# Copies of the transposed k, in a linear-attention and mixture-of-experts kernel: from VectorE to ScalarE

## The chip, the cores and the metric

The kernel runs on one core of one Trainium2 chip. The metric is the time of one execution on the device, in microseconds (us). The engines are named as the profile names them: PE (TensorE, the matmuls), PEld (its weight loads), DVE (VectorE), ACT (ScalarE), POOL (GpSimd) and SP (SyncE, which here only issues transfers). Each engine carries out its own instructions in the order in which they stand in its program, and waits on semaphores for what other engines have to deliver. PSUM is the memory into which PE writes, in eight banks; SBUF is the large on-chip memory.

## The reference

Four batches of 512 tokens with 256 channels pass through two blocks, all in float32, each with a residual and a layer norm in front.

```python
q = k = x @ Wqk + bqk                  # 16 heads of 16 channels
v, u  = silu(x @ Wv + bv), silu(x @ Wu + bu)
q, kh = elu(heads(q)), elu(heads(k))
kv    = einsum('bhnd,bhne->bhde', kh, vh)
out   = einsum('bhnd,bhde->bhne', q, kv)
x     = x + (u * layernorm(out)) @ Wo + bo
...
gate  = einsum('bsd,de->bse', layernorm(x), gate_kernel)   # 8 experts, the best 2 of them
inter = silu(h0) * h1                                      # hidden width 512
x     = x + einsum('bse,bsem,emd->bsd', combine, inter, wo_kernel)
```

The attention has no softmax over the tokens: each head's k and v are first multiplied over all 512 tokens of a batch into a 16 by 16 matrix kv, and q is then multiplied by it. q and k are the same numbers here.

## The kernel before, in words

**Attention.** `attention(b)` is a generator with twelve stages for one batch; the four batches start four stages apart and run interleaved, the later batch's stage first. The stages that the text speaks of, with their lines:

- The layer norm of x (`layernorm`, L247 to L286): statistics with L252 and L253, a chain of ten tiny DVE operations for the reciprocal root (L255 to L272, each waiting for the one before), then four normalizations, L284 on DVE for tokens of even blocks and L280 on ACT for odd ones. POOL then adds bo to x (L305).
- x is transposed on PE (L292) and copied by ACT (L297).
- k and q: PE multiplies (L317), ACT takes the exponential (L322), DVE makes elu of it (L323, L324). The result kT has channels on the partitions and tokens along the free dimension.
- v and the gate logits (L346, L351, L354, L358), and u (`project`, L334, L338).
- kn, k with tokens on the partitions: PE transposes kT (L391) into a PSUM bank, two blocks of 128 tokens at a time, and **L394 copies the bank to SBUF**. There are two such copies a batch, eight in all, each of 128 partitions by 512 floats. For batch 0 the gate's own small products stand in the same stage (L380 to L410).
- kv: PE multiplies kn and v (L421, with kn as weights), DVE masks it (L429).
- the attention output o: L442 on PE, L446 on ACT; its layer norm, with the same lines as the first; transposed (L292), scaled by ACT (L457) and multiplied by u on DVE (L461).
- the output projection L469 on PE, the residual L473 on DVE, and the result's transfer to the output, issued by ACT (L476).
- the routing: the two best experts (L498, L499, L502, L508), the third layer norm into hn, whose rows POOL doubles (L511), the exponential of the second weight (L516), then L518 to L520.
- the places: PE counts the tokens of each expert up to here (L524, L526), DVE makes row numbers (L530, L533) and counts (L535), and POOL scatters hn to the DRAM buffer xg with eight indirect transfers a batch (L539).

**Experts.** When two batches are routed, `plan` (L658) makes the list of the first blocks of 128 rows. For a block, SP fetches the rows from xg (L715), which has to wait until the scatters of the batches it depends on have landed; PE transposes them (L726), ACT copies (L729), expert weights at a place known only at run time are staged by ACT and DVE copies (L741), and PE multiplies (L759, then silu L843 and product L778, then L798). DVE weights the result (L809), and POOL adds it to the output with an indirect transfer (L819). The third expert matrix, w2, is loaded by SP (L174) into the arena slots that attention used, each load as soon as the slot's last reader is done.

**What sets the order.** The source's order is not the order on the engines: the tile framework schedules the instructions of each engine by its own estimate of their costs, and inserts the waits. So moving one operation to another engine can also reorder others. PSUM banks are handed out in turn by `bank`, and a bank's next writer waits for its last reader.

```python
for t0 in range(0, NT, 2):                              # L387
    ps = bank([P, 2, E], f"knp_{b}_{t0}")
    for t in range(t0, t0 + 2):
        for c in range(EC):
            nc.tensor.transpose(ps[:, t - t0, bass.ts(c, P)], kT[:, c, bass.ts(t, P)], ident)
    nc.vector.tensor_copy(kn[:, t0 : t0 + 2, :], ps)    # L394
```

Of the kernel before, what the change touches and what calls it, by code (L numbers as in the profile page):

```python
# [32 lines left out]
def kernel(  # L33
# [32 lines left out]
    nc = tc.nc  # L66
# [29 lines left out]
    def bank(shape, name, n=1):  # L96

        at = (used[0] + used[0] % n) % BANKS
        used[0] = (at + n) % BANKS
        if n == 2:  # L100
            return banks[:, at : at + 2, 0 : shape[2]]
        tile_ = banks[:, at, 0 : math.prod(shape[1:])]
        if len(shape) == 3:
            tile_ = tile_.rearrange("p (a b) -> p a b", a=shape[1])
        return tile_
# [9 lines left out]
    def att(tag):  # L115

        i = turns[tag] % COUNT[tag]
        turns[tag] += 1
        if tag == "kv":
            return arena[:, AT[tag], bass.ts(i, E)]  # L120
        return arena[:, AT[tag] + i, :]
# [177 lines left out]
    def attention(b):  # L299
# [14 lines left out]
        for c in range(EC):  # L314
            ps = bank([P, N], f"qp_{b}_{c}")
            for k in range(EC):
                nc.tensor.matmul(  # L317
                    ps, lhsT=wqk_sb[:, k, bass.ts(c, P)], rhs=xT[:, k, :],
# [23 lines left out]
        for t0 in range(0, NT, 2):  # L342
            ps = bank([P, 2, E + NE], f"vp_{b}_{t0}", 2)
# [18 lines left out]
        if b == 0:  # L362

            ps = bank([P, NE], "gate_sum")
            for k in range(EC):
                nc.tensor.matmul(
                    ps, lhsT=ones, rhs=wv_sb[:, k, E:], start=(k == 0), stop=(k == EC - 1)
# [9 lines left out]
            ps = bank([P, EC, E], "woTp")  # L377
# [8 lines left out]
        kn = att("tok").rearrange("p (t e) -> p t e", t=NT)  # L386
# [4 lines that stand above are left out]
                    nc.tensor.transpose(  # L391
                        ps[:, t - t0, bass.ts(c, P)], kT[:, c, bass.ts(t, P)], ident
                    )
            nc.vector.tensor_copy(kn[:, t0 : t0 + 2, :], ps)  # L394
        if b == 0:

            ps = bank([P, EC + 1, NE], "wog")
# [18 lines left out]
        ps = bank([P, EC, HALF], f"kvp_{b}")  # L416
# [21 lines left out]
        for t0 in range(0, NT, 2):  # L438
            ps = bank([P, 2, E], f"op_{b}_{t0}")
# [25 lines left out]
        for t0 in range(0, NT, 2):  # L465
            ps = bank([P, 2, E + NE], f"ap_{b}_{t0}", 2)
# [26 lines left out]
        ps = x1[:, :, E:]  # L493
# [364 lines left out]
    W2_AT = 9  # L858
    begin = [0, 4, 8, 12]
    running = [attention(b) for b in range(B)]  # L860
    ready = []
    for at in range(max(begin) + STAGES + 1):
# [37 lines left out]
    with tc.If(many > USUAL - EARLY):  # L900
# [7 lines left out]
        for name, some in (  # L908
# [8 lines left out]
            for b in range(B):  # L917
# [10 lines left out]
                for t in range(NT):  # L928
                    ps = bank([P, E], f"spread_{name}_{b}_{t}")
                    for k in range(NT):  # L930
                        nc.tensor.matmul(
                            ps, lhsT=at[k][:, bass.ts(t, P)], rhs=state["made"][:, k, :],
# [49 lines left out]
```

## Time and profile before

| What | Value |
|---|---|
| Median of 3 runs | 327.46 us (326.52 to 327.5) |
| The profiled execution | 326.6 us |
| its span, first to last instruction | 324.8 us |
| mean granted TensorE clock | 0.964 |
| PE busy | 293.6 us (90%) |
| DVE busy | 157.0 us (48%) |
| ACT busy | 127.1 us (39%) |
| POOL busy | 121.7 us (37%) |
| the chain that ended last | PE 73%, DVE 19%, ACT 3% |

The profile is of one execution, and all its times are us from the start of its span. A row of a group gives the source line, the engine, the operation, the tile written and the tiles read, and how often; then the durations. In an answer in order of time, the first column is the start and the second the duration, and a bracket tells how long the engine had stood and what it waited for. Two operations of one engine can overlap by their pipelines, so an operation's duration is a little more than the time for which it keeps its engine from the next. The chain of work that ended last is followed back from the last instruction: at each step to what released it, or to the instruction before it on its engine; its second column is the time that the step adds to the chain.

Attention fills the first 115 us or so, and the experts' matmuls the rest. The share of DVE and ACT over the whole span says little about attention, where DVE is the fullest engine for long stretches.

### The profile page before, as it was taken

To read this page: it belongs to the slowest core of one execution; us is meant where nothing else is said; L and a number is where in the kernel's file an instruction comes from. 1 tells how busy PE (TensorE), PEld (TensorE's weight loads), DVE (VectorE), ACT (ScalarE), POOL (GpSimd) and SP (SyncE) were. 2 spreads that over 40 slices of the span, in tenths; PEclk is the share of its full clock that TensorE was granted. 3 is DMA by queue.
4 is the path that set the end of the run, shared out by engine and by line. 5 is a ranking of instruction groups with operands and counts; after the bars stand their busy time and mean duration, and the time that the engine had idled before them with its cause. 6 is when DMAs were issued, how large, how long until landed. Compare 5 with 4: busy or idle time off the path is not lost.

```text
span 324.8 us, 5819 instructions
## 1 busy us (share of the span) xinstructions
PE 293.6 (90%) x1948; PEld 235.9 (73%) x1948; DVE 157.0 (48%) x567; ACT 127.1 (39%) x203; POOL 121.7 (37%) x161
## 2 busy tenths in 40 slices
PE   0999999899794599999999999999999999999970
PEld 0567677576663389899974456758999999999960
DVE  5653979979968466843221232332232323233320
ACT  2465566357341835524212144334242424343200
POOL 5340041176461553752331343323343224332321
PEclk9999999999996579999999999999999999999996
DMA  6999403054168450734433122232323433322121
GB/s 199 329 387 385 174 2 109 22 163 163 36 227 266 123 197 9 225 83 64 68 52 54 18 34 35 33 44 33 59 29 63 60 55 61 58 33 34 18 34 20
DMA packets 27731, 32.98 MB, mean 102 GB/s; under 512 B 3249, under 2 KB 22577, under 8 KB 27697
## 3 DMA queue, kind: packets, MB, share of 16 engines
q1 hardware_dynamic: 19056, 21.73, 21.4%
q0 software_dynamic: 6528, 8.72, 16.3%
q10 hardware_dynamic: 2112, 2.10, 1.9%
q8 instruction: 18, 0.29, 0.4%
q14 instruction: 17, 0.13, 0.1%
HBM read 20.53 MB, written 12.01 MB: 100 GB/s over the span
## 4 chain that ended last, share of the span: by engine, by line
PE 73%; DVE 19%; ACT 3%; issue 1%; DMA 1%; POOL 0%; POOLq 0%; DVEq 0%; ACTq 0%
PE banks L759 28%; PE banks L798 19%; PE banks L767 7%; PE banks L469 4%; DVE st L252 4%; PE banks L317 3%; PE banks L726 3%; PE banks L292 2%; PE banks L346 2%; DVE x L473 1%; PE banks L334 1%; PE banks L421 1%; PE banks L785 1%; DVE mv L253 1%; ACT arena L457 1%
## 5 line engine op out<-in xcount | busy, mean ns | idle before, releaser
L759 PE MATMUL banks<-arena 128*128 128x128 f32 x896 | 108.8, 275 | 0.1
L759 PEld LDWEIGHTS banks<-arena 128*128 128x128 f32 x896 | 106.2, 192 | 1.6 <-ACT arena L741 0.3
L729 ACT COPY arena<-banks 128x256 f32<-128x256 f32 x34 | 12.6, 372 | 102.7 <-PE banks L726 102.7
L819 POOL DMA_INDIRECT out_dram<-ys_full,g_full x19 | 30.0, 1577 | 59.5 <-issue 25.7
L539 POOL DMA_INDIRECT xg<-hn,idx_i x32 | 32.0, 999 | 16.9 <-issue 8.5
L798 PE MATMUL banks<-arena,it_full 128*128 x152 | 36.3, 381 | 0.9 <-DVE it_full L778 0.9
L741 ACT COPY arena<-w_sb 128x1024 f32 x30 | 31.3, 1046 | 3.0 <-DVE arena L461 0.8
L798 PEld LDWEIGHTS banks<-arena,it_full 128*128 128x128 f32 x152 | 27.4, 190 | 5.6 <-issue 1.6
L809 DVE TENSOR_SCALAR ys_full<-banks,g_full 128x256 f32<-128x256 f32 x19 | 9.2, 483 | 46.1 <-PE banks L798 46.1
L778 DVE TENSOR_TENSOR it_full<-s_full,banks 128x512 f32<-128x512 f32 x19 | 13.1, 688 | 29.9 <-PE banks L759 29.9
L767 PE MATMUL banks<-w_sb,arena 128*64 128x512 f32 (+1 forms) x80 | 23.2, 605 | 0.0
L819 POOL DMA_INDIRECT out_dram<-ys_early,g_early x9 | 14.1, 1563 | 22.3 <-issue 6.7
L741 DVE COPY arena<-w_sb 128x1024 f32 x30 | 21.4, 712 | 0.9 <-DVE arena L461 0.5
L292 PE MATMUL banks<-ident,arena 128*128 128x128 f32 x64 | 11.2, 317 | 10.5 <-DVE arena L284 8.4
L469 PE MATMUL banks<-wo,arena 128*128 128x264 f32 x64 | 17.5, 434 | 1.4 <-DVE arena L461 1.4
L819 POOL DMA_INDIRECT out_dram<-ys_last,g_last x8 | 11.7, 1463 | 16.9 <-issue 7.9
L798 PE MATMUL banks<-arena,it_early 128*128 x72 | 17.3, 384 | 0.6 <-DVE it_early L778 0.6
L292 PEld LDWEIGHTS banks<-ident,arena 128*128 128x128 f32 x64 | 8.3, 162 | 12.4 <-issue 8.2
L305 POOL TENSOR_TENSOR x<-x,bo 128x256 f32<-128x256 f32 x16 | 12.5, 813 | 12.9 <-DVE arena L284 12.9
L469 PEld LDWEIGHTS banks<-wo,arena 128*128 128x128 f32 x64 | 13.4, 217 | 4.5 <-DVE arena L461 1.8
L317 PE MATMUL banks<-arena,wqk 128*128 128x512 f32 x32 | 16.2, 652 | 0.0
L346 PE MATMUL banks<-wv,arena 128*128 128x264 f32 x64 | 15.7, 397 | 0.0
(212 smaller groups left out, 417.2 us busy)
## 6 DMA issues: line engine op xcount, KB each, us to landing
w_sb<-in_w_dram SPq DMA_DIRECT2D x16, 512.0 KB, 10.8
arena<-in_w_dram SPq DMA_DIRECT2D x8, 512.0 KB, 5.2
g_full<-xg SPq DMA_DIRECT2D x19, 130.0 KB, 2.1
out_dram<-x ACTq DMA_DIRECT2D x4, 512.0 KB, 3.1
x<-in_x_dram SPq DMA_DIRECT2D x3, 512.0 KB, 5.7
xg<-empty SPq DMA_DIRECT2D x9, 130.0 KB, 3.7
g_early<-xg SPq DMA_DIRECT2D x9, 130.0 KB, 3.6
g_last<-xg SPq DMA_DIRECT2D x8, 65.0 KB, 2.1
```

Source lines behind the costliest of these rows:

```text
L252: nc.vector.bn_stats(out=st, in_=src[:, t, :])
L292: nc.tensor.transpose(ps[:, bass.ts(t, P)], src[:, t, bass.ts(c, P)], ident)
L317: nc.tensor.matmul(ps, lhsT=wqk_sb[:, k, bass.ts(c, P)], rhs=xT[:, k, :], start=(k == 0), stop=(k == EC - 1),)
L346: nc.tensor.matmul(ps[:, t - t0, :], lhsT=xT[:, k, bass.ts(t, P)], rhs=wv_sb[:, k, :], start=(k == 0), stop=(k == EC - 1),)
L469: nc.tensor.matmul(ps[:, t - t0, :], lhsT=yT[:, c, bass.ts(t, P)], rhs=wo_sb[:, c, :], start=(c == 0), stop=(c == EC - 1),)
L539: apart(nc.gpsimd.indirect_dma_start(out=xg[:, :], out_offset=bass.IndirectOffsetOnAxis(ap=idx_i[:, t, k : k + 1], axis=0), in_=hn[:, t, k ...
L741: copy(w[i][0], hidden_w2[i][:, bass.ds(at, OW)])
L759: nc.tensor.matmul(ps[:, m, :], lhsT=t[:, bass.ds(at + k * M + m * P, P)], rhs=gT[:, k, :], start=(k == 0), stop=(k == EC - 1),)
L767: nc.tensor.matmul(ps.rearrange("p m n -> p (m n)")[here, :], lhsT=gT[:, k, here], rhs=t[:, bass.ds(at + k * M, M)], start=(k == 0), stop= ...
L778: nc.vector.tensor_tensor(it, s, ps, ALU.mult)
L798: nc.tensor.matmul(ps[here, :], lhsT=it[:, m, here], rhs=t[:, bass.ds(at + m * E, E)], start=(m == 0), stop=(m == MC - 1), tile_position=N ...
L819: ins = nc.gpsimd.indirect_dma_start(out=whole[:, :], out_offset=bass.IndirectOffsetOnAxis(ap=g[0 : P // len(w), E + 1 + u : E + 2 + u].bi ...
```

## The change

The copies of k with tokens on the partitions are made by ACT in place of DVE. Shape, source, destination and number stay.

```diff
@@ -391,7 +391,7 @@
                     nc.tensor.transpose(
                         ps[:, t - t0, bass.ts(c, P)], kT[:, c, bass.ts(t, P)], ident
                     )
-            nc.vector.tensor_copy(kn[:, t0 : t0 + 2, :], ps)
+            nc.scalar.copy(kn[:, t0 : t0 + 2, :], ps)
         if b == 0:
```

In the program as it is built, other instructions change their places with it. On ACT, the copies of batch 1 and of batch 2 stand ahead of the scalings L457 of the batch before, those of batch 3 behind the second L358. On DVE, the four statistics (L252) of the last batch's attention output come after L530 of batch 2, where they stood before it, and the list of the first blocks (L664 to L619) is interleaved otherwise. On SP, the sixth load of w2 stands ahead of the first fetch of a block, where it stood behind the second. POOL's order is the same.

## The prediction

> **What bounds the kernel now.** I read the page's slices first, then the chain that ended last in order of time, then the copies' own rows, then the stretch around 100 us by engine. The profiled execution took 326.6 us, 324.8 of it span and 1.8 outside it. The page's slices (8.12 us each, digits in tenths):
>
> ```profile
> PE   0999999899794599999999999999999999999970
> DVE  5653979979968466843221232332232323233320
> ACT  2465566357341835524212144334242424343200
> PEclk9999999999996579999999999999999999999996
> ```
>
> Counted from 0, PE is full from slice 14 (114 us) to the tail: whatever moves the start of that stretch moves the end by as much. Before it DVE is at 9 in many slices while ACT is half idle; PE drops in slices 12 and 13, its clock in 12 to 14. All eight changed copies lie before 87 us. They can matter only by when the dense PE stretch starts, with the last output projection (L469 of batch 3) at 112.08 us. The copies' row, and the chain where it runs through them (start, us, what):
>
> ```profile
> L394 DVE COPY arena<-banks x8: 655/680/692, 24.4 to 86.2; 128x512 f32<-128x512 f32 x8
> ```
>
> ```profile
> 63.24 0.59 DVE arena L394
> 63.97 0.61 DVE arena L394
> ...
> 85.65 0.57 DVE arena L394
> 86.30 0.59 DVE arena L394
> ```
>
> Only four of the eight are on the chain, 2.36 us together; batch 0's and batch 1's are not. The stretch before the last projection, on PE, and the clock there (columns of the second: us, busy us of PE, PEld, DVE, ACT, POOL, granted clock, DMA share, GB/s):
>
> ```profile
> 99.94 0.64 PE L726 MATMUL banks<-ident,g_early 128*128 128x128 f32 x2 [2.71 <-DVE st L252]
> ...
> 104.50 1.09 PE L726 MATMUL banks<-ident,g_early 128*128 128x128 f32 x4 [1.98 <-DMA g_early<-xg]
> ...
> 112.08 6.26 PE L469 MATMUL banks<-wo,arena 128*128 128x264 f32 x16 [1.38 <-DVE arena L461]
> ```
>
> ```profile
> 97.20:99.90 2.70, 0.04 (x1) 0.00 (x0) 2.70 (x21) 0.59 (x1) 0.40 (x4) 1.00 0.50 131
> 99.90:112.00 12.10, 6.47 (x26) 4.95 (x26) 6.53 (x40) 6.38 (x12) 4.05 (x8) 0.50 0.64 202
> 112.00:117.00 5.00, 4.92 (x11) 3.88 (x12) 2.32 (x7) 1.99 (x2) 3.79 (x4) 0.50 0.68 208
> ```
>
> PE stands from 97.2 to 99.94. The profile names a DVE statistic, but the first L726 needs the first fetched block: SP issued that fetch at 97.46, when the last of POOL's eight scatters of batch 1 (L539, 85.83 to 95.92) had landed. So between 86 and 100 us a second chain runs beside the chain of DVE work: idx of batch 1 (L533, DVE, 85.37), eight scatters at 1.28 us, landing, fetch, L726. DVE time saved after 85.4 us cannot shorten it.
>
> **The change, part by part.** DVE loses eight copies. A DVE copy blocks its engine for about 0.60 us (0.57 to 0.61 on the chain). ACT gains eight; the nearest row is L446, the same 128x512 from PSUM on ACT, 0.586 us, and an ACT operation behind it starts after 0.51. ScalarE: Activation LUTs, Rules for kernel authors, speaks against the change: plain arithmetic belongs on VectorE, up to about 3 times faster per element (in bf16). By that rule each copy might take some 2 us (an estimate, 3 times 0.68), 4 us a batch in ACT's row; by L446 and L394, f32 out of PSUM, ACT is the faster by 0.1. I take 0.51. A copy on ACT loads no table in the trace (L446, L729), and the built order of the changed kernel has as many table loads as before, so none is added. What counts is where the copies stand in ACT's order, batch by batch.
>
> Batch 0: they stand behind the copy of woT (ends 24.56), so they end near 25.7, as on DVE; the kv matmuls L421 start at 26.96. Worth 0, hidden by the gate matmuls and transposes of 24.8 to 27.0; without that cover 0.1.
>
> Batch 1: in ACT's new order both copies stand behind the normalizations of x of batch 2 (L280) and ahead of L457. DVE gains: the last steps of that layer norm lose the 1.2 us between them but keep a step of 0.20, so L272 moves from 42.71 to 41.79. ACT: L280 at 42.17 and 42.67, copies at 43.16 and 43.67, L457 at 44.18 where it had been 42.67. Then L461 waits for L457, at 45.0. POOL's four additions L305 (0.73 each, about 0.70 apart), released by that layer norm, now run from 42.5 to 45.3 and hold L461 a little: it ends at 45.9. PE: L421 ends at 45.2, L469 starts at 46.0 where it had been 45.33. Cost **+0.65** at L473 (47.93), which DVE's unbroken row carries on. ACT's copies are queued ahead of L457, and DVE, then PE, wait for that: this is the new wait.
>
> Batch 2 (times before the 0.65): without copies L272 comes at 63.61 in place of 64.68, and the rest of both layer norms 1.08 earlier. ACT's copies end at 63.95 and fit ahead of L280. L457 ends at 68.0 (before 68.89), L461 lets L469 start at 68.14 in place of 68.71: **-0.57**, and DVE reaches L473 of batch 1 that much earlier.
>
> Does that survive? At 74.32 POOL starts the next four L305. They stand behind scatters that start from idx (L533 at 62.88, ahead of the copies in DVE's order), so they don't come earlier. In that stretch L502 took 0.65 us where its twin of batch 0 took 0.21 at 51.23, and L508, L514 and L255 stretched too, each to the end of one L305: from L502 to L262 it took 2.88 us against 1.31 in batch 0. SBUF — State Buffer, section SBUF: two separate sides, says why: the port pair of DVE and GpSimd is an exclusive lock, held for a whole instruction. By the rule four small DVE operations are stopped whether DVE comes 0.57 earlier or not, and only 0.1 is kept past 77.1 us; by plain subtraction 0.57 is. I take the rule, since the rows show one stop in each L305: so far +0.65 - 0.10 = **+0.55** (other end +0.08).
>
> Batch 3: ACT's copies run at 85.0 to 86.1 behind L358, while PE is busy with L334 until 86.4; the projection of batch 2 comes 1.5 us earlier (L284 of that layer norm 88.3, not 89.5; L461 at 90.2, not 91.8). But PE then waits for the fetch instead. And the built order puts L533 behind two operations more and an L253, 0.28 later. The scatter chain moves by +0.55 + 0.28 = **+0.83**.
>
> Behind the fetch two edits of order oppose each other. DVE: the four statistics of batch 3's attention output (L252, 0.33 each) now stand behind L530, which waits for L726; from L530 to L284 it takes 5.4 us in place of 3.6 (102.56 to 106.16). SP: one load of w2 (512 KB, issued at 98.87 between the second and third fetch) goes ahead of all fetches, where its last reader is done near 89.4, 8 us before the first fetch can go; nothing waits behind it, so it costs 0. The third and fourth fetch go near 99.2 and 100.0, not 100.36 and 101.18, so ACT's L729 end near 104.4, not 106.0. ACT then waits for DVE's L272 (L530 + 2.6 + 0.25 = 105.4, before 106.0), takes two L280, a table load of 1.28 and L516, and reaches the last L280 at 108.05 in place of 108.52; DVE's part is ready at 108.0. Sum here **-0.45**: the longer DVE row is hidden by ACT's table load, with nothing to spare.
>
> Sum: +0.83 - 0.45 = +0.38 at L469 of batch 3. The clock returned at 117.0; if it returns then again, a later start loses half of that, since the work moved out of this stretch ran at half speed: +0.2 to +0.4. I take **+0.3**: span 325.1, execution 326.9; the median shown is 327.46, 0.86 over the profiled execution, so **327.8 us**.
>
> **The rivals.**
>
> *Freed DVE time reaches the end (faster).* DVE is the fullest engine up to 87 us, and 2.36 us of copies are on its chain. All of it falling through gives 324.2 for the execution, 325.1 as median. Against it: the scatter chain starts ahead of batch 3's copies (1.16), so at most batch 2's 1.2 counts. If batch 1 costs nothing and batch 2's 0.57 survives: -0.57 + 0.28 - 0.45 = -0.74, so 326.7; with a whole 1.2, 326.1. Chance of faster by over 0.3% (0.98 us, about what a measurement here can tell from no change): 0.17.
>
> *The clock returns later (slower).* The granted clock was 0.50 from 99.9 to 117.0, and returned 4.9 us after PE became dense at 112.08. TensorE: Matmul & The Clock Gate, Part 1, has it return after a window of about 3.4 us of sustained work; this trace shows one return, not the window's grid. By that rule a start up to about 113.6 still returns at 117.0, and one behind it at 120.4. The decisive point is a shift of 1.5 us at L469, which the longer DVE row alone (1.8) can reach if ACT doesn't come earlier. Price: 3.4 us more at half speed is 1.7, with half of the shift before it some 2.5: 330.0. For it: the order was built with L530 ahead of the statistics. Against: the fetches come earlier. A part of that row showing without the clock gives +1 to +1.5. Slower by over 0.3%: 0.35.
>
> *The forecast*, within 0.3%: 0.48; its own range 326.5 to 328.4. The range for 8 in 10 is 326.2 to 330.0: its low end is the first rival, its high end the second.
>
> **What would show it.** Right: the 128x512 copies on ACT near 0.58; L457 of batch 0 near 44.2; L469 of batch 0 near 46.0; L502 of batch 1 or L508 behind it still stretched; the projection of batch 2 about 1 us earlier; the first L726 near 100.8; L469 of batch 3 within 1 us of 112.1. Wrong: the first L726 well before 99.9 (the scatters start earlier than I think), L305 no longer stopping DVE, or the clock's return after 118.

## The result, and the profile after

The changed kernel takes 327.82 us, the kernel before 325.99 us (medians of 20 runs each; 325.79 to 330.53 and 325.14 to 327.5). The ratio is 1.0055, with a 95% interval of 1.0038 to 1.0072: slower by 0.55%, or 1.8 us. The three runs of before that the forecast started from, 327.46, 327.5 and 326.52, are the two slowest of those twenty and the sixth. So 327.8 was met as a time, and missed as a difference: +0.3 was forecast. That the time agrees is luck: the base was 1.5 us too high, and the loss was forecast 1.5 us too small. In the runs below, an execution over 1.5% above the fastest of its kernel counts as slow; the medians are of all runs, the ratios of the fast ones alone.

The profiled execution after took 328.53 us, its span 326.8. The page's slices (8.17 us each):

```profile
PE   0999989999895299999999999999999999999960
DVE  5832959969963766853221233332232323233320
ACT  2565657647431645524312144334242424243200
PEclk9999999999796579999999999999999999999995
```

PE's hole is deeper than before (5 and 2 in slices 12 and 13, where 4 and 5 stood before), and the clock has an additional dip in slice 10. The same three stretches as before (us, busy us of PE, PEld, DVE, ACT, POOL, granted clock, DMA share, GB/s):

```profile
97.20:99.90 2.70, 0.06 (x1) 0.00 (x0) 1.39 (x11) 0.88 (x2) 0.53 (x5) 1.00 0.70 245
99.90:112.00 12.10, 5.81 (x25) 4.95 (x26) 6.73 (x37) 5.04 (x10) 2.13 (x5) 0.56 0.47 132
112.00:117.00 5.00, 3.62 (x10) 2.58 (x9) 2.06 (x3) 3.44 (x4) 3.89 (x4) 0.50 0.68 185
```

DVE has now 1.39 us of work between 97.2 and 99.9, where it had been full: it too waits. DMA moves 245 GB/s there, not 131.

The copies themselves, min, median and max in ns, and ACT's and PE's rows of batch 1 in order of time:

```profile
L394 ACT COPY arena<-banks x8: 567/588/603, 23.4 to 85.0; 128x512 f32<-128x512 f32 x8
```

```profile
42.11 1.05 ACT L394 COPY arena<-banks 128x512 f32<-128x512 f32 x2
43.05 1.46 ACT L457 ACTIVATE arena<-banks,cols 128x512 f32<-128x512 f32 x2
...
44.92 3.83 PE L469 MATMUL banks<-wo,arena 128*128 128x264 f32 x16 [0.79 <-DVE arena L461]
```

A copy takes 0.588 us, as L446 did (0.586). Then the stretch that decides, in the chain that ended last (start, us, what):

```profile
95.11 4.09 DMA xg<-hn,idx_i
...
99.22 2.11 DMA g_early<-xg
...
101.46 0.66 PE banks L726 x2
...
102.39 1.68 PE banks L526 x8
...
104.09 0.07 DVE at L530
...
110.12 0.42 DVE arena L284
...
113.94 2.12 PE banks L469 x4
```

The chain of before, in the same place:

```profile
102.56 0.07 DVE at L530
...
108.61 0.50 ACT arena L280
...
112.08 4.33 PE banks L469 x9
```

In before the chain does not run through the landing. What SP and POOL issued there, in before and then after (the last of the eight scatters of batch 1, the loads of w2, the first fetches):

```profile
94.95 0.97 POOL L539 DMA_INDIRECT xg<-hn,idx_i  x1 [0.30 <-issue]
88.02 0.92 SPq L174 DMA_DIRECT2D arena<-in_w_dram  x2
97.46 1.23 SPq L715 DMA_DIRECT2D g_early<-xg  x2
98.87 0.73 SPq L174 DMA_DIRECT2D arena<-in_w_dram  x1
```

```profile
95.11 0.97 POOL L539 DMA_INDIRECT xg<-hn,idx_i  x1 [0.31 <-issue]
88.94 1.59 SPq L174 DMA_DIRECT2D arena<-in_w_dram  x3
99.22 2.89 SPq L715 DMA_DIRECT2D g_early<-xg  x4
```

The two executions are shifted against each other before the first changed copy: the first eight L317 took 4.20 us in one and 5.27 in the other, though nothing ahead of them differs. So times are best compared from the first L317 of batch 1 on (27.01 after, 28.05 before), called the origin from here on. Only batch 0's two copies lie ahead of it, and they cost nothing: from the end of batch 0's L317 to the origin it takes 11.50 us in both. From the origin, in us:

| Event | before | after | later by |
|---|---|---|---|
| L469 of batch 0 | 17.28 | 17.91 | 0.63 |
| L469 of batch 1 | 40.66 | 40.67 | 0.01 |
| first scatter L539 of batch 1 | 57.78 | 58.64 | 0.86 |
| last of these eight starts | 66.90 | 68.10 | 1.20 |
| first fetch goes (it has landed) | 69.41 | 72.21 | 2.80 |
| first L726 | 71.89 | 74.45 | 2.56 |
| L530 of batch 2 | 74.51 | 77.08 | 2.57 |
| first L284 of the layer norm of batch 3's attention output | 78.11 | 83.11 | 5.00 |
| L469 of batch 3 | 84.03 | 86.93 | 2.90 |
| end of the span | 296.79 | 299.76 | 2.97 |

Up to the first scatter all goes as forecast (+0.86, where +0.83 was written). The loss comes in the 14 us behind it, up to the first fetch, and what is lost at L469 of batch 3 is lost at the end.

### The profile page after: what moved, and what is told of

It is laid out like the page before. It is cut to its first block, busy times and chain, and to the rows that moved or that the text cites. A ratio compares the mean times of both kernels' runs of the same rounds, so it can differ in the third digit from the quotient of the medians.

```text
span 326.8 us, 5819 instructions
## 1 busy us (share of the span) xinstructions
PE 293.9 (90%) x1948; PEld 235.9 (72%) x1948; DVE 152.8 (47%) x559; ACT 130.7 (40%) x211; POOL 123.7 (38%) x161
## 4 chain that ended last, share of the span: by engine, by line
PE 70%; DVE 8%; POOL 2%; issue 2%; DMA 2%; ACT 0%; POOLq 0%; DVEq 0%; ACTq 0%
PE banks L759 30%; PE banks L798 19%; PE banks L767 7%; PE banks L469 4%; PE banks L726 3%; POOL xg L539 2%; PE banks L292 1%; DMA xg<-hn,idx_i 1%; DVE st L252 1%; PE banks L346 1%; PE banks L334 1%; PE banks L317 1%; PE banks L526 1%; PE banks L785 1%; PE banks L421 1%
## 5 line engine op out<-in xcount | busy, mean ns | idle before, releaser
L729 ACT COPY arena<-banks 128x256 f32<-128x256 f32 x34 | 12.6, 372 | 102.3 <-PE banks L726 102.2
L539 POOL DMA_INDIRECT xg<-hn,idx_i x32 | 33.6, 1050 | 17.9 <-issue 8.2
L778 DVE TENSOR_TENSOR it_full<-s_full,banks 128x512 f32<-128x512 f32 x19 | 13.1, 687 | 30.5 <-PE banks L759 30.5
L292 PE MATMUL banks<-ident,arena 128*128 128x128 f32 x64 | 11.1, 320 | 12.9 <-DVE arena L284 12.7
L469 PE MATMUL banks<-wo,arena 128*128 128x264 f32 x64 | 17.5, 432 | 2.2 <-DVE arena L461 2.2
L819 POOL DMA_INDIRECT out_dram<-ys_last,g_last x8 | 12.1, 1512 | 16.6 <-issue 7.9
L469 PEld LDWEIGHTS banks<-wo,arena 128*128 128x128 f32 x64 | 13.3, 213 | 6.0 <-DVE arena L461 3.4
L334 PE MATMUL banks<-arena,wu 128*128 128x512 f32 x32 | 16.5, 653 | 1.0 <-DVE x L354 1.0
L305 POOL TENSOR_TENSOR x<-x,bo 128x256 f32<-128x256 f32 x16 | 11.7, 760 | 11.4 <-DMA bo<-in_bo_dram 7.4
```

Of the source, the lines that this page charges most:

```text
L292: nc.tensor.transpose(ps[:, bass.ts(t, P)], src[:, t, bass.ts(c, P)], ident)
L334: nc.tensor.matmul(ps, lhsT=wu_sb[:, k, bass.ts(c, P)], rhs=xT[:, k, :], start=(k == 0), stop=(k == EC - 1),)
L469: nc.tensor.matmul(ps[:, t - t0, :], lhsT=yT[:, c, bass.ts(t, P)], rhs=wo_sb[:, c, :], start=(c == 0), stop=(c == EC - 1),)
L539: apart(nc.gpsimd.indirect_dma_start(out=xg[:, :], out_offset=bass.IndirectOffsetOnAxis(ap=idx_i[:, t, k : k + 1], axis=0), in_=hn[:, t, k ...
L729: nc.scalar.copy(gT, ps)
L778: nc.vector.tensor_tensor(it, s, ps, ALU.mult)
```

## The experiments

The theory after the result (A): the sixth load of w2, now ahead of the fetches, fills the DMA engines while the scatters are in flight. The last scatter's landing, counted here from its start to the first fetch, comes late, and the fetch, L726, L524 and L526 behind it on PE, and L530 wait. The rival (B): the landing is hidden; the loss is L530's new place ahead of four statistics. A third (C) came with the first runs: the loss is that of batch 1's copies alone. Each ratio is to the kernel before, on the same chip, with its 95% interval.

**One batch alone, and the load held back.** The first three have copies on ACT in one batch only, the fourth is the changed kernel with another order on SP:

```diff
-            nc.vector.tensor_copy(kn[:, t0 : t0 + 2, :], ps)
+            (nc.scalar.copy if b in (1,) else nc.vector.tensor_copy)(kn[:, t0 : t0 + 2, :], ps)
```

with (1,), (2,) or (3,). The fourth:

```diff
@@ load_w2, changed kernel
-            nc.sync.dma_start(
+            ins = nc.sync.dma_start(
...
+            for i in {5: (1,)}.get(e, ()): tc.add_manual_dep(ins.ins, state["fetch"][i].name, mybir.DependencyInfo(mybir.DependencyClass.NoSync, mybir.DependencyReason.DATA), reason="order")
@@ fetch
-            tc.add_to_no_dep_group("reads", ins.ins)
+            tc.add_to_no_dep_group("reads", ins.ins); state["fetch"].append(ins.ins)
```

Batch 1 alone. 

> Only batch 1's two copies are on ACT; the built order differs from before only around 42 us (DVE's two copies gone, L457 behind the copies on ACT). Both theories: L457 of batch 0 later, L469 of batch 0 +0.65 us, carried to the end by DVE's unbroken row and the scatters, so +0.4 to +0.7 us over before. If the 0.65 doesn't reach the end: 0.

Measured: 328.28 against 326.42 us, 1.005 (1.0031 to 1.007). From the common origin L469 of batch 0 is late by 0.63, as forecast, once 1.12 is taken off for batch 1's L317, which took 4.82 us here in place of 3.70. The clock was at half there, in a stretch that ran at full clock in the profile before (columns as above):

```profile
28.10:31.40 3.30, 3.30 (x27) 2.13 (x22) 0.42 (x1) 1.66 (x3) 0.00 (x0) 0.50 1.05 385
```

The mechanism is as forecast, but the ratio says 1.6 us, the medians 1.9, where the trace explains 0.63; its execution, 329.56, is the slowest of the six. That was (C)'s start.

Batch 2 alone. 

> Only batch 2's two copies are on ACT. The built order also puts the sixth load of w2 ahead of the first fetch and L533 of batch 1 behind a few operations more; L530 of batch 2 stays behind the statistics of batch 3, as before. Theory A (the sixth load fills the DMA engines while POOL's scatters are in flight, so the last one lands late): fetch about 1.5 us later behind the last L539, first L726 later, +0.8 to +1.5 us over before. Theory B (L530 ahead of the statistics lengthens DVE's row): nothing of that here, the L457 gain of 0.6 mostly lost to L305, so -0.5 to +0.2.

Measured: 325.16 us, 0.996 (0.9945 to 0.9975). Faster, against theory A's sign, and the whole interval (0.8 to 1.8 us under before) lies outside B's range as well. Its chain:

```profile
94.75 3.48 DMA xg<-hn,idx_i
...
98.25 2.44 DMA g_early<-xg
...
103.45 0.07 DVE at L530
...
107.34 0.42 DVE arena L284
...
111.16 4.91 PE banks L469 x11
```

The landing is late (3.5 us), as A says, and the first L726 with it: 1.58 us later from the common origin. But four fetches now go together, so ACT's L729 are done at 104.8 and not 106.0, and with L530 still behind the statistics the row from L530 to L284 takes 3.9 us. L726 to L469 falls from 12.1 to 10.3 us. From the origin L469 of batch 3 is early by only 0.22 and the end by 0.15, so the profiled execution explains 0.15 of the 1.3 us that the medians differ by; its earlier front (27.35) is no part of the change.

Batch 3 alone. 

> Only batch 3's two copies are on ACT. The built order has both the sixth load of w2 ahead of the first fetch and L530 of batch 2 ahead of the statistics of batch 3. Theory A: last scatter lands about 4 us after it starts in place of 2.5, +1.0 to +1.6 us over before. Theory B: L530 to the last L284 of the hidden layer norm takes 6 us in place of 3.6, about +0.7. Neither: 0.

Measured: 326.85 us, 1.0007 (0.9984 to 1.0029), at most 0.9 us over before: less than A's 1.0, while B's 0.7 and no change both lie in the interval. The trace has both, a landing of 3.4 us and a row of 6.0 from L530 to L284, and the gain of the early fetches against them. L469 of batch 3 is late by 0.13 from the origin. Both theories had left out that gain.

The sixth load held back. 

> All copies on ACT as in the changed kernel; only SP's order differs: the sixth load of w2 stands behind the second fetch, as before the change, and the seventh behind the third. Theory A: last scatter lands near 2.5 us after it starts, first L726 about 1.5 us earlier than in the changed kernel, time 326.3 to 326.8 (-1.0 to -1.5 against the changed kernel). Theory B: the fetches are not what bounds, time as the changed kernel, +1.5 to +2 over before.

Measured: 326.56 us, 1.002 (1.000 to 1.0039); of the changed kernel's 0.55%, 0.35 is gone with one place on SP (the two intervals, 0 to 0.39% and 0.38 to 0.72%, barely touch). The chain, and the DMA share (last column but one) while the last scatter is in flight, in before, in the changed kernel and here:

```profile
95.08 2.62 DMA xg<-hn,idx_i
...
100.46 0.41 PE banks L726 x2
...
101.93 0.06 DVE at L530
...
107.95 0.42 DVE arena L284
...
111.77 3.85 PE banks L469 x8
```

```profile
95.00:97.40 2.40, 2.24 (x14) 1.82 (x12) 2.37 (x12) 0.13 (x1) 0.92 (x1) 1.00 0.34 120
```

```profile
95.00:97.40 2.40, 2.26 (x13) 1.37 (x11) 2.40 (x18) 0.49 (x2) 0.97 (x1) 1.00 1.02 381
```

```profile
95.00:97.40 2.40, 2.23 (x13) 1.33 (x11) 2.40 (x18) 0.53 (x2) 0.97 (x1) 1.00 0.45 159
```

The landing is back at 2.6 us, and the DMA engines, full in the changed kernel, are not here, while DVE (2.40) and POOL (0.97) are as busy in both. The row from L530 to L284 stays at 6.0. A holds for the landing, and B for a second part.

**Two batches out of three, and the loads of w2 behind the fetches.** Batch sets (0, 1, 2) and (0, 2, 3) by the same line. For the other two, in the kernel before and with batch 2's copies on ACT, the fifth to eighth load go behind the fourth fetch (the edit ties the sixth and seventh; in the built order the fifth goes there too):

```diff
-            load_w2()
-
+            load_w2(range(5))
+        if at == begin[B - 1] + W2_AT + 2: load_w2(range(5, NE))
...
+            for i in {5: (3,), 6: (3,)}.get(e, ()): tc.add_manual_dep(...)
```

Batch 3's copies left on DVE. 

> Copies of batches 0, 1 and 2 on ACT, batch 3's on DVE. Against the changed kernel L530 of batch 2 is back behind the statistics of batch 3; the sixth load of w2 stays ahead of all fetches. Theory (batch 1 costs 0.65 and the DVE row behind L530 costs 2 once the fetches come early): time = batch 2 alone + 0.65, so about 0.6 us under before, 325.8. Rival (the loss is batch 1's alone, near 1.9 as its own run gave): about as the changed kernel less nothing, +0.6 over before or more.

Measured: 326.54 against 326.31 us, 1.0007 (0.9987 to 1.0027). Between the two expectations: the interval takes in the rival's +0.6 us and not the theory's -0.6, while the one profiled execution (325.01, among the fastest) has L469 of batch 3 early by 0.65 from the origin. Of the changed kernel's 0.55%, 0.5 is gone.

Batch 1's copies left on DVE. 

> Copies of batches 0, 2 and 3 on ACT, batch 1's on DVE. Against the changed kernel only the stretch around 42 us differs. Theory: the changed kernel less 0.65, +0.7 to +1.2 over before, since the sixth load and the DVE row stay. Rival (batch 1 carries the loss): the changed kernel less 1.9, so no slower than before.

Measured: 326.64 us, 1.0009 (0.9991 to 1.0028). Also 0.5% better than the changed kernel; the interval takes in the low end of the theory (+0.7 us) and the rival's no loss, so it does not decide. So taking back batch 1, or batch 3, or one load each removes most of the loss, while the three alone give 0.50 - 0.40 + 0.07 = 0.17%. The parts do not add, if only just by their intervals, and (C) is not the whole.

Loads behind, copies on DVE. 

> All copies on DVE as before the change; the fifth to eighth load of w2 stand behind the fourth fetch, so the four fetches go together. If the gain of batch 2's run comes from the fetches going together (no load between them), the third and fourth fetch are some 3 us earlier, ACT is no longer late, and L469 of batch 3 starts 1.5 to 2 us earlier: -1.3 to -2.0 against before. If it comes from the copies, 0.

Measured: 325.3 us, 0.9952 (0.9925 to 0.9979). As expected in time: L469 of batch 3 is early by 1.7 from the origin, L726 to L469 takes 10.5 us and not 12.1, and the last scatter lands in 2.5. The third and fourth fetch go only 0.5 us earlier from the origin, not some 3; but with no load between the fetches the second block's L726 starts 1.7 earlier. So the gain of batch 2's run can be had by SP's order, without a copy on ACT.

Loads behind, batch 2 on ACT. 

> Batch 2's copies on ACT and the fifth to eighth load of w2 behind the fourth fetch. If the loads ahead of the fetches delay the landing of the scatters (theory A), the last scatter lands 2.5 us after it starts in place of 3.5 and L469 of batch 3 starts about 1 us earlier than with batch 2's copies alone: -2.0 to -2.5 against before. If DVE or ACT bounds that stretch anyway: as batch 2 alone, -1.3.

Measured: 326.33 us, 0.9997 (0.9977 to 1.0017): a miss. The landing is 2.45 us, and L469 of batch 3 stands 1.9 us earlier from the origin, as expected. From L469 to the end, though, it takes 213.7 us, where it takes 212.8 in before: the clock came back 6 us behind L469's start, not 4.9. That explains 0.9 us in the one profiled execution; for the median it is not shown.

**PE no longer waits for the fetch.** If the loss runs through scatter, landing, fetch and L726, then putting L524 and L526 of batch 2 ahead of the first L726 on PE should make the landing harmless:

```diff
-            nc.tensor.matmul(
+            state["pos"] = nc.tensor.matmul(
                 pos[:, d:, :], lhsT=ones, rhs=mask[:, 0 : NT - d, :], start=False, stop=(d == NT - 1)
@@ turn
-            nc.tensor.transpose(ps[:, c, :], g[:, bass.ts(c, P)], ident)
+            ins = nc.tensor.transpose(ps[:, c, :], g[:, bass.ts(c, P)], ident); tc.add_manual_dep(ins.ins, state["pos"].ins.name, ...)
```

Changed copies. 

> All copies on ACT as in the changed kernel; on PE the position matmuls of batch 2 (L524, L526) stand ahead of the first L726, so they and L530 no longer wait for the fetch. If the loss of the change comes through scatter, landing, fetch, L726 and L530: L530 starts near 98.6 in place of 104.1, its DVE row of 6.0 us ends near 104.6, L469 of batch 3 starts about 5 us earlier, and what sets it no longer depends on where the copies are: 4 to 5 us under the changed kernel. If the loss is batch 1's alone: 0 to -2.

Copies on DVE. 

> All copies on DVE, the same order on PE. L530 no longer waits, but the third fetch still goes at 102.5 behind a load of w2, so the third L726 (104.5) holds L292 and L469: about 3 us under before. Against the changed kernel with the same order: if the loss came through the fetch, no slower or slower than it by up to 2; if it came from batch 1's copies or from the clock, still faster than it by about 1.5.

Batch 2's copies on ACT. 

> Batch 2's copies alone on ACT, the same order on PE. L292 waits for the third fetch only (back to back with the first, so near 101.5 to 103), L469 near 107 to 108: 4 to 5 us under before, and 0 to 0.7 under the changed kernel with this order, by batch 1's 0.65.

Measured: 342.46, 342.03 and 342.38 us against 341.61, so 1.002 (0.9995 to 1.0045), 0.9996 (0.9968 to 1.0024) and 1.0011 (0.9987 to 1.0035). These three say little on the theories, since on that chip the kernel before itself takes 15 us more, and the stretch has another bound. In the chain of the first of them:

```profile
67.26 3.50 another core or an unknown queue
```

DVE stood 3.5 us ahead of L429 there, ACT 7.7 ahead of L457 from 90 us on, and DVE 8.6 ahead of L778 from 140 us on, for nothing that the trace can name in the program. L469 of batch 2 starts at 99.8 in place of 91.7, and the first L726 follows L526 without a wait: here the fetch bounds nothing.

The same kernel as the first of the three, once more, on a chip where before takes 326. 

> The same kernel as the one with the changed copies and L524, L526 ahead of the first L726, once more, since the kernel before took 341.6 us beside it, 15 more than in the other runs, and DVE, PE and ACT stood together near 68 and 91 us for reasons that neither theory covers. Where the kernel before takes about 326: by the theory of the fetch, L530 starts near 98.6, L469 of batch 3 near 108.5, and the time is 3 us under before (4 to 5 under the changed kernel). If batch 1's copies carry the loss: 0 to 1 over before. Where the kernel before takes about 341 again: no difference, within 0.3%.

Measured: 322.82 against 326.02 us, **0.9898** (0.9872 to 0.9924).

```profile
97.69 0.41 PE banks L524 x2
98.10 0.89 PE banks L526 x8
...
99.01 0.07 DVE at L530
...
103.59 1.09 ACT hn L280 x2
...
109.45 3.52 PE banks L469 x8
```

L530 starts at 99.0, not 104.1, though the last scatter still needs 3.1 us to land and the first L726 stands at 100.7. L469 of batch 3 is 4.9 us earlier from the origin than in the changed kernel (82.0, not 86.9), and ACT's table load sets it. All eight copies are on ACT here, batch 1's too. With the wait for the fetch gone this kernel beats both. Whether the copies still cost anything under this order is not shown: the kernel before with the same order ran only on the chip of 341.6 us, where the two differ by less than their intervals.

## Why the prediction was right and wrong, by its steps

**Right in the batches.** Copies near 0.58 (0.588 measured). L457 of batch 0 waits behind the copies, L469 is 0.63 late (+0.65 forecast). Batch 2 wins 0.62 (0.57 forecast) and keeps nothing: again four small operations of DVE were stretched, each to the end of one of POOL's four L305, now L508, L514, L255 and L261 (0.32, 0.73, 0.56 and 0.70 us), where it was L502, L508, L514 and L255 before, and L262 stands +0.56 late (+0.55). The lock of the port pair, taken from the Trainium skill (SBUF — State Buffer, section SBUF: two separate sides) and the rows, was the right choice over plain subtraction here. First scatter +0.86 (+0.83). One mark missed here: the projection of batch 2 came 0.13 earlier from the origin and not about 1, since L334 fell into the dip of the clock (3.68 us for four, not 1.98). Behind the scatters the forecast's own marks tell against it: L469 of batch 3 came at 113.94 and not within 1 us of 112.1, and the clock returned at 118.3, which it had named as a sign of being wrong.

**The step that failed:** "one load of w2 (512 KB, issued at 98.87 between the second and third fetch) goes ahead of all fetches, ...; nothing waits behind it, so it costs 0." Nothing waits behind it on SP's queue, but the scatters share the 16 DMA engines with it. From the last scatter's start to the first fetch it took 2.5 us before and 4.1 after: +1.60 in a term priced at 0. Held behind the second fetch, the landing takes 2.6. Over all runs where before takes 326, it is 2.45 to 2.64 us in the five kernels that issue at most five loads ahead, and 2.8 to 4.1 in the six that issue six; the two groups do not overlap. (The 2.8 is from an execution of 329.65 us, 3 us over the median of its kernel, batches 0, 2 and 3; the next is 2.9.) Why it is 4.1 in one of those six and 2.8 in another is not settled. In the changed kernel's profile three loads go together at 88.94, since the fourth waits for L421, which came behind a dip of the clock (84.2 to 87.6); with no dip, in the last kernel, they went from 87.5 on and the landing took 3.1.

The scatters' own row grew by 0.34 as well (9.46 us from first to last start, not 9.12), also priced at 0. The fifth scatter took 1.33 us there and not 0.98. The load is not the cause: with six loads ahead the row is 9.07 and 9.08 in batch 2 alone and batches 0, 1 and 2, and 9.36 to 9.47 only where batch 3's copies are on ACT too. What stretched that scatter is not shown.

**A second term, mis-sized.** L530 to L284 was put at 5.4 us, "hidden by ACT's table load, with nothing to spare". It took 6.0, since POOL's L511 (1.56 us without a gap) stopped four small operations, at about 0.3 us each and not 0.17. It is not hidden: DVE's L272 released ACT's last L280.

```profile
107.34 1.56 POOL L511 COPY hn<-hn 128x256 f32<-128x256 f32 x4 [7.45 <-DVE hn L284]
107.51 0.39 DVE L261 TENSOR_SCALAR nt<-var 128x4 int32<-128x4 int32 x1
...
108.94 0.16 DVE L267 SCALAR_TENSOR_TENSOR nt<-nt 128x4 f32<-128x4 f32 x1
...
110.18 1.09 ACT L280 ACTIVATE arena<-arena,nt,rs 128x256 f32<-128x256 f32 x2 [0.69 <-DVE nt L272]
```

Together, from L530 on, the forecast had -0.45 and the trace +0.33 (5.92 us from L284 to L469 before, 3.82 after; +2.43 - 2.10).

The sum by these terms is 0.86 + 0.34 + 1.60 + 0.33, less 0.23 between fetch and L530: +2.90, where +0.38 was forecast. The medians show 1.8. One profiled execution of each kernel, with a dip of the clock in one of them, is not a median: with a landing of 3.1, as in the last kernel without a dip, the sum would be 1.9 (an estimate). How often the dip comes is not known, so the difference between 2.9 and 1.8 stays open.

**The rivals.** Slower by a longer DVE row was named, and its decisive point, a shift of 1.5 at L469, was passed; its price was wrong. It counted on a return of the clock 3.4 us later. The half clock lasted 17.1 us in both (99.96 to 117.03 and 101.25 to 118.32, worked out from the granted clock in stretches of 1.5 us): it began later and ended later. The forecast's own discount, that a later start loses half of its shift, failed in the same way: L469 to the end takes 212.8 us in both. The rival of a gain that reaches the end is refuted for the whole change, though batch 2 alone was faster by 0.4%.

**Open:** that batch 1's copies cost 1.6 to 1.9 us over all runs and 0.63 in the trace, and that the parts do not add. Single executions differ by more than these parts: from the end of batch 0's L317 to the origin it takes 11.5 us in both before and the changed kernel, but 12.7 in the profile of batch 1 alone and 12.9 in that of batches 0, 2 and 3, which have the same copies of batch 0 as one of these two. Part of the second is shown: batch 2 brings the early fetches, which pay as long as L530 keeps its place, and batch 3 takes that place.

## What to carry to other kernels

A transfer that is moved ahead in an idle queue is not free: ask what else is in the DMA engines until it has landed, above all a small transfer that the next step waits for. Where an engine works in order, look what stands behind an instruction that waits for a transfer; here the small matmuls L524 and L526 behind the first L726 tied the last attention to a fetch it does not need, and moving them was worth more (1.0% under before) than the change cost. And take the time before from many runs: the median of the first three was 1.5 us above that of all twenty, nearly the whole effect.

## What the hardware showed

In these traces the half clock lasts whole multiples of 3.41 us: 3.42 (four single dips), 10.2 (the last kernel), 13.6 to 13.7 (five kernels), 17.1 (before, changed, batch 1 alone, batch 2 alone, batches 0, 2 and 3), each worked out from the granted clock in stretches of 1 or 1.5 us. The Trainium skill (TensorE: Matmul & The Clock Gate, Part 1) gives a free-running window of that length. The traces agree: the two dips of the changed kernel begin 17.1 us apart (84.2 and 101.3), five windows, while the long dip begins anywhere from 98.6 to 103.2 in the eleven kernels. The forecast had tied the return to the program's time. One such window of dense PE work at half speed costs up to 1.7 us, half of it (four L334 took 3.68 us in one, 1.98 without), and runs of one kernel differ by that and more.

One chip took 15 us more than the others for the same kernel before (341.6 and 326). The three traces from it, of kernels with the new order on PE, have stretches where DVE, ACT and PE stand for nothing that the trace names in the program, one of them of some 9 us at 140 us; that these make up the 15 us is not shown.
